# Cross-attention block in float32: pairs of fc split over a unit's border, with products joined in TensorE's accumulators

## The chip, the cores and the metric

The kernel runs on one core of a Trainium2 chip. The core has five engines that run side by side, each through its own list of instructions in order: TensorE (PE, matmuls into PSUM), VectorE (DVE), ScalarE (ACT), GpSimd (POOL) and SyncE (SP, which here issues most DMAs). They wait for each other by semaphores. The metric is the time of one execution on the device in microseconds; a profile, taken of one execution, shows what each engine did.

## The reference

Four batches of 512 rows of 512 numbers, all in float32. What is computed, with layer norm's affine part and all biases kept:

```python
x = layer_norm(hidden, ln1_w, ln1_b)
q = (x @ q_w + q_b)                      # 16 heads of 32
k, v = (enc @ k_w + k_b), (enc @ v_w + v_b)
attn = softmax(q @ k.T / sqrt(32))       # masked
hidden = hidden + (attn @ v) @ cproj_w + cproj_b
y = layer_norm(hidden, ln2_w, ln2_b)
y = gelu(y @ fc_w + fc_b)                # 512 -> 2048, tanh form
out = hidden + y @ proj_w + proj_b       # 2048 -> 512
```

## The kernel before, in words

The work has two stages. In the first, attention goes by *windows*: a window `w` is one batch and four heads (16 windows), and each has four *units*, one for each 128 queries, so there are 64 units; unit `u` is window `u // 4`, quarter `qt = u % 4`. A unit does `scores(w, qt)`: four matmuls on TensorE into one PSUM tile `sc` (L262), for each head a minimum on VectorE that copies the scores out (L266) and an exponential on ScalarE (L270). Then `turn(w, qt)`: transposes on VectorE (L285), and in odd units a reciprocal of the sums (L290), its copy `rr` on ScalarE (L292) and two more transposes (L293, L294). SyncE's DMAs exchange blocks of the result (L328), and some units later `attend` multiplies by the values (L345, tile `av`) and VectorE scales it (L350, `oT`). The tile `sc` has one buffer, so the next scores wait for the fourth minimum of the unit before.

Between these pieces stands other work, so that TensorE has something to do while VectorE and ScalarE are at the scores: projections for coming windows (`prep_k`, `prep_q`, `prep_v`: L218, L228, L240), the output projection `cproj` (L386), layer norms with their transposes (`tp`, L159), and the MLP of the batches 0 and 1. Which item follows which unit is written out by hand in the lists `first` and `later`: for a tuple, entry `qt` holds the items that follow the scores of that unit; for a list, the items are dealt over the window's four units by their costs. `some(n)` takes the next MLP items from the list `mlp`, in which a chain counts 1 and a pair 2. The program order of an engine is the order in which these Python functions are called.

The MLP's first product (`fc`) has two forms. `fc(b, f)` is a chain: four matmuls 128x512 into an accumulator, then gelu on ScalarE (L537), for 128 of the 2048 columns. Batch 1's first half of the columns goes this way (8 chains, in the units 57 to 63). `fc_by_pair(b, c)` takes two such column blocks at once by `fc_seven`: a 2x2 block product in seven half-width products in place of eight (Strassen's scheme in Winograd's form). Its inputs are sums of blocks: of the weights (`a_sums`, by POOL in the first stage through `fc_sums`, by VectorE in the second through `sum_wa`), and of the normed input (`y_sums`). Each product is two matmuls 128x256 (L495). Before, the seven products go to four accumulators, and the results are combined outside of PSUM: ScalarE copies the first product (L498), VectorE adds twice by 512, once by 256 and once more by 512 (L455), and ScalarE applies gelu to two blocks of 512 (L513).

The accumulators `acc` are a pool of four PSUM banks for everything in the first stage but `sc`. The second product `proj` (L554) multiplies by the lower weights and adds to `hid` on VectorE (L558). Weights of the MLP go through a ring of eight places that `load_mlp` refills when their last reader is done.

The second stage, `last_mlps`, has no attention left: half of batch 1's MLP, then batches 2 and 3, again by pairs, one directly after the other, with `project` for the second product, also by seven products (L622). There the four banks of `sc` have become a second pool (`half_tile`), and SyncE loads a pair's weights (`load_wa`, L578) when the pair before the last is done with the place.

ScalarE holds one table of functions at a time; where an exponential follows a gelu, or the reverse, a table load stands between them (ACT_TABLE_LOAD).

Of the kernel before, what the change touches and what calls it, by code (L numbers as in the profile page):

```python
# [20 lines left out]
P = 128  # L21
# [31 lines left out]
def xattn_block(ctx: ExitStack, tc: tile.TileContext, x, encT, mask, q_w, k_w, v_w, c_w, fc_w, p_w, vecs, rows, out):  # L53
# [342 lines left out]

    def load_hid(b, ts_):

        for t in ts_:
            if ("hid", b, t) not in S:  # L400
                S["hid", b, t] = hids.tile([P, D], F32, tag="hid", name=f"hid_{b}_{t}")
            Q[0].dma_start(out=S["hid", b, t], in_=S["xa", b][ts(t, P), :])
        for t in ts_:
            add_row(S["hid", b, t], 1)
# [46 lines left out]
    def sub(o, x0, x1, engine=None):  # L451
        (engine or nc.vector).tensor_tensor(o, x0, x1, ALU.subtract)  # L452

    def add(engine, o, x0, x1):
        engine.tensor_tensor(o, x0, x1, ALU.add)  # L455
# [16 lines left out]
    def y_sums(b):  # L472
        y11, y12, y21, y22 = y_blocks(b)
        e = nc.vector if b else nc.gpsimd
        sub(ys[:, 0], y12, y11)
        sub(ys[:, 1], y22, ys[:, 0])
        sub(y12, y22, y12, e)
        sub(ys[:, 2], y21, ys[:, 1], e)

    def acc_half(name):  # L480
        return acc_tile(name).rearrange("p (i l) -> p i l", i=2)

    def fc_seven(b, c, g, a, s, half):

        y11, t3, y21, y22 = y_blocks(b)
        t1, t2, t4 = (ys[:, i] for i in range(3))
        s1, s2, s3, s4 = s
        q1, q26 = (acc_half(f"{n}_{b}_{c}") for n in ("q1", "q26"))
        q57, q34 = (half(f"{n}_{b}_{c}") for n in ("q57", "q34"))
        p1 = small.tile([P, HL], F32, tag="p1", bufs=1, name=f"p1_{b}_{c}")  # L490
        g = g.rearrange("p i (j l) -> p (i j) l", j=2)

        def product(o, x, y):
            for k in range(2):
                nc.tensor.matmul(o, x[:, k], y[:, k], start=(k == 0), stop=(k == 1))  # L495

        product(q1[:, 0], a[0][:, 0:2], y11)
        nc.scalar.copy(p1, q1[:, 0])  # L498
        product(q26[:, 0], a[0][:, 2:4], y21)
        product(q26[:, 1], s2, t2)  # L500
        add(nc.vector, g[:, 0:4:3], q26, p1[:, None, :].broadcast_to([P, 2, HL]))
        product(q57[:, 1], s3, t3)
        product(q57[:, 0], s1, t1)
        u2 = g[:, 3:4]
        add(nc.vector, g[:, 1:3], q57, u2.broadcast_to([P, 2, HL]))
        add(nc.vector, g[:, 3], q57[:, 0], g[:, 2])
        product(q34[:, 0], s4, y22)
        product(q34[:, 1], a[1][:, 2:4], t4)
        add(nc.vector, g[:, 1:3], q34, g[:, 1:3])
        for i in range(2):  # L510
            f = 2 * c + i
            h = g[:, 2 * i : 2 * i + 2]
            nc.scalar.activation(h, h, AF.Gelu_apprx_tanh, bias=vec[:, FCB + f : FCB + f + 1], scale=1.0)  # L513

    fc_pairs = [(b, c) for b in range(SPLIT) for c in range(NP)]

# [3 lines left out]
    def fc_sums():  # L520

        while count[3] < len(fc_pairs) and count[3] < count[4] + 2:
            b, c = fc_pairs[count[3]]
            if ("fcw", b, 2 * c + 1) not in S:
                return
            x, y = raw_pair(b, c)
            s = wsum[:, count[3] % 2]
            a_sums(x[:, :2], x[:, 2:], y[:, :2], y[:, 2:], s[:, 0], s[:, 1], y[:, :2], s[:, 2], nc.gpsimd)
            S["ws", b, c] = s[:, 0], s[:, 1], y[:, :2], s[:, 2]
            count[3] += 1  # L530

    def fc(b, f):
        q, k = divmod(f, FQ)
        acc = acc_tile(f"accf_{b}_{f}")
        for d in range(ND):
            nc.tensor.matmul(acc, S["fcw", b, f][:, d, :], S["yT", b][:, d, :], start=(d == 0), stop=(d == ND - 1))  # L536
        nc.scalar.activation(  # L537
            gT[q % 2][:, k, :], acc, AF.Gelu_apprx_tanh, bias=vec[:, FCB + f : FCB + f + 1], scale=1.0
        )
        count[1] += 1  # L540
        load_mlp()

    def fc_by_pair(b, c):
        q, k = divmod(2 * c, FQ)
        fc_seven(b, c, gT[q % 2][:, k : k + 2, :], raw_pair(b, c), S["ws", b, c], acc_half)
        count[1] += 2
        count[4] += 1
        load_mlp()
        fc_sums()
# [40 lines left out]
    def last_mlps():  # L590
# [17 lines left out]
        def fc_pair(b, c, sums):  # L608
            sums()
            fc_seven(b, c, ga[:, c], [wa[c % 2][:, i] for i in range(2)],  # L610
                     [ws[c % 2][:, i] for i in range(4)], half_tile)

        def project(b, pairs, sums, turns, middle):
# [51 lines left out]
            for t in range(2):  # L665
                product(q4[t], g22, t4, (t,))
                add(nc.vector, hid(1, 0, t), q4[t][:, t], hid(1, 0, t))
                nc.sync.dma_start(out=out[b, ts(2 + t, P), :HL], in_=hid(1, 0, t))

        y_sums(SPLIT)  # L670

# [48 lines left out]
    def do(fn):  # L720
        return [(0.0, fn)]
# [19 lines left out]
    def FC(b, q):  # L741
        if b < SPLIT:
            return [(2 * CHAIN * 7 / 8, lambda c=c: fc_by_pair(b, c)) for c in range(q * FQ // 2, (q + 1) * FQ // 2)]
        return [(CHAIN, lambda f=f: fc(b, f)) for f in range(q * FQ, (q + 1) * FQ)]

# [71 lines left out]
    def some(n):  # L817
        taken = []
        while n > 0:
            n -= 1 if mlp[0][0] == CHAIN else 2  # L820
            taken.append(mlp.pop(0))
        assert n == 0
        return taken

    def hid_(b, *ts_):
        return do(lambda: load_hid(b, ts_))

# [15 lines left out]
    def norm(b, *ts_):  # L843
# [9 lines left out]
    first[5] = (  # L853
        [k] + stat(0, 0, 1, 2, 3) + rs(0) + do(fc_sums) + x3 + norm(0, 0, 1, 2, 3) + [v], [q] + t2 + do(lambda: y_sums(0)), some(2) + pb_(0), some(2)
    )
    k, q, v = A(9)
    x1, x2, x3, x4 = inputs(3)
    first[6] = [k, q] + some(4) + [v] + x1
    k, q, v = A(10)
    first[7] = [k, q] + x2[:1] + some(2) + x2[1:2] + some(2) + [v]  # L860

    k, q, v = A(11)
    first[8] = h_(1, 0, 1) + x2[2:] + [k, q] + x3[:2] + some(2) + x3[2:3] + [v] + x3[3:] + h_(1, 2, 3) + x4
    later[8] = cb(1) + C(1)
    k, q, v = A(12)
    first[9] = [q] + some(2) + [k] + some(2) + [v]
    k, q, v = A(13)
    first[10] = [k, q] + some(4) + [v]
    k, q, v = A(14)
    t2 = turns2(1)  # L870
    first[11] = (
        [k, q] + stat(1, 0, 1, 2, 3) + rs(1), some(2) + norm(1, 0, 1, 2, 3), some(1) + t2[:2] + [v],
        t2[2:] + pb_(1) + some(1) + h_(2, 2, 3, 0, 1)
    )

    k, q, v = A(15)
    c = C(2)
    first[12] = [k, q], cb(2) + [v], c[:2], c[2:]
    first[13] = some(1), some(1) + stat(2, 0, 1), some(1) + stat(2, 2, 3) + rs(2), some(2)
    first[14] = some(1) + norm(2, 0, 1), some(1) + norm(2, 2, 3), some(2), some(1)  # L880
    first[15] = hid_(1, 2, 3) + some(1), some(1), some(1), some(2)

    for w in range(NW):
        if w and w % NG == 0:
            make_mb(w // NG)

        work, rest = first[w], later[w]
        by_unit = isinstance(work, tuple)
# [88 lines left out]
```

## Time and profile before

| what | us |
|---|---|
| runs | 802.65, 802.84, 805.95 (median 802.84) |
| profiled execution, its own time | 801.93 |
| span in the profile | 800.2 |
| TensorE busy | 785.3 |
| VectorE busy | 573.8 |
| ScalarE busy | 339.5 |
| POOL busy | 123.9 |

The span runs from the first to the last instruction; the execution's time holds some 1.7 us around it. A line of the timeline gives start, duration, engine, source line, operation and tiles; lines of the same kind that follow each other are merged (x8 is a pass each of eight: a float32 matmul shows as two), and the bracket at the end tells of idle time before it and of what ended it. TensorE's ends are modelled, so starts are the safer reading: a pair's length is read from its start to the next item's start. A line of the waits gives who waited for whom, the total, how often and the longest. The first stage ends at about 549.6 us, where the first pair of the second stage starts. In a unit without disturbance the first minimum starts 1.21 after its scores, the first exponential 1.94, and the fourth ends 4.78 after them (units 20, 22, 25 and others).

### The profile page before, as it was taken

What the parts mean: (1) busy time and instruction counts of PE and PEld (TensorE: products, weight loads), DVE (VectorE), ACT (ScalarE), POOL (GpSimd) and SP (SyncE); (2) the same over time, 40 slices, a digit from 0 to 9 for tenths busy, and PEclk for the clock granted to TensorE, in tenths of its full rate; (3) what the DMA queues carried; (4) which work ended last, traced back from release to release, by engine and by line L of the source; (5) the groups of instructions that cost most, each with busy time, mean ns of one, the idle gap of its engine ahead of it and who ended that gap; (6) DMA issues with size and microseconds to landing.
All of it is one profiled execution on the core that took longest, in us unless ns stands there. A gap on an engine that the chain in (4) does not pass through costs nothing.

```text
span 800.2 us, 12085 instructions
## 1 busy us (share of the span) xinstructions
PE 785.3 (98%) x4178; PEld 499.4 (62%) x4178; DVE 573.8 (72%) x1179; ACT 339.5 (42%) x745; POOL 123.9 (15%) x146
## 2 busy tenths in 40 slices
PE   9999999989999999999999999999999999999998
PEld 6545455456655645556553433446888888888887
DVE  3789998888888857779878988546738983368511
ACT  2567765547763636456554479500201220022100
POOL 1210030055121141001220100020040020200011
PEclk9999999999999999999999999999999999999999
DMA  8889999847897777787777799882325330033001
GB/s 325 289 230 241 235 237 244 231 115 182 209 240 196 211 210 192 179 198 199 181 173 213 205 261 246 202 254 93 117 84 172 118 106 14 27 86 86 1 14 40
DMA packets 60957, 137.15 MB, mean 171 GB/s; under 512 B 12464, under 2 KB 15664, under 8 KB 60768
## 3 DMA queue, kind: packets, MB, share of 16 engines
q1 hardware_dynamic: 59472, 132.43, 61.3%
q0 software_dynamic: 896, 2.82, 1.1%
q10 hardware_dynamic: 528, 1.14, 0.7%
q8 instruction: 33, 0.54, 0.3%
q14 instruction: 28, 0.23, 0.1%
HBM read 58.22 MB, written 6.82 MB: 81 GB/s over the span
## 4 chain that ended last, share of the span: by engine, by line
PE 87%; DVE 6%; SPq 3%; ACT 1%; issue 1%; DMA 1%; POOL 0%; DVEq 0%; POOLq 0%; ACTq 0%
PE q L495 20%; PE accp L554 8%; PE sc L262 7%; PE accc L386 7%; PE av L345 7%; PE accv L240 6%; PE acck L218 6%; PE accq L228 5%; PE accf L536 3%; DVE ptt L266 3%; SPq L328 2%; PE q4p L622 2%; PE q3p L622 2%; PE q5p L622 2%; PE q6p L622 2%; PE q7p L622 2%
## 5 line engine op out<-in xcount | busy, mean ns | idle before, releaser
L270 ACT ACTIVATE ptt<-ptt,mn 128x512 f32<-128x512 f32 x256 | 181.7, 711 | 135.1 <-DVE mn L266 134.8
L266 DVE CUSTOM_DVE_ANT_0 ptt<-sc,mb 128x512 f32<-128x512 f32 x256 | 161.0, 685 | 32.7 <-PE sc L262 32.4
L285 DVE STREAM_TRANSPOSE tb<-ptt 128x1024 f32<-128x1024 f32 x96 | 119.2, 1242 | 14.4 <-ACT ptt L270 12.9
L554 PE MATMUL accp<-pbt,gt 128*128 128x512 f32 x192 | 86.7, 600 | 0.0
L495 PE MATMUL q<-yT,gt 128*128 128x256 f32 x320 | 78.9, 379 | 0.0
L262 PE MATMUL sc<-pbt 32*128 32x512 f32 x512 | 73.0, 640 | 4.7 <-DVE mn L266 2.5
L513 ACT ACTIVATE ga<-ga,vec 128x512 f32<-128x512 f32 x40 | 26.7, 714 | 93.2 <-DVE ga L455 93.2
L495 PEld LDWEIGHTS q<-yT,gt 128*128 128x128 f32 x320 | 60.8, 190 | 8.7 <-issue 0.5
L554 PEld LDWEIGHTS accp<-pbt,gt 128*128 128x128 f32 x192 | 35.2, 190 | 49.0 <-issue 46.4
L240 PEld LDWEIGHTS accv<-ptt,xe 128*128 128x128 f32 x512 | 58.7, 192 | 9.5 <-issue 6.7
L495 PE MATMUL q<-ys,gt 128*128 128x256 f32 x240 | 61.8, 380 | 0.5 <-DVE ys L452 0.5
L240 PE MATMUL accv<-ptt,xe 128*128 128x128 f32 x512 | 60.8, 277 | 0.0
L218 PE MATMUL acck<-xe,ptt 128*128 128x512 f32 x128 | 59.1, 605 | 0.0
L228 PE MATMUL accq<-xe,ptt 128*128 128x512 f32 x128 | 58.4, 599 | 0.0
L386 PE MATMUL accc<-wc,oT 128*128 128x512 f32 x128 | 56.6, 596 | 0.0
L495 PEld LDWEIGHTS q<-ys,gt 128*128 128x128 f32 x240 | 45.4, 190 | 7.4 <-DVE ys L452 0.9
L345 PE MATMUL av<-pT,v 128*32 128x256 f32 x768 | 48.1, 392 | 1.8 <-DMA gt<-tb 0.7
L498 ACT COPY p<-q 128x256 f32<-128x256 f32 x28 | 9.9, 355 | 92.5 <-PE q L495 92.5
L270 ACT ACTIVATION_READ_ACCUMULATOR ptt<-ptt,mn 128x1 f32 x256 | 47.8, 187 | 0.0
L252 POOL TENSOR_TENSOR v<-v,row 128x512 f32<-128x512 f32 x16 | 20.4, 1275 | 172.9 <-ACT v L245 172.8
L228 PEld LDWEIGHTS accq<-xe,ptt 128*128 128x128 f32 x128 | 23.6, 190 | 32.4 <-issue 30.4
L262 PEld LDWEIGHTS sc<-pbt 32*128 32x128 f32 x512 | 20.0, 182 | 37.9 <-issue 21.4
(137 smaller groups left out, 1071.4 us busy)
## 6 DMA issues: line engine op xcount, KB each, us to landing
pT<-tb SPq DMA_DIRECT2D x384, 136.0 KB, 2.4
pbt<-p_w_dram SPq DMA_DIRECT2D x40, 256.0 KB, 3.1
gt<-fc_w_dram SPq DMA_DIRECT2D x40, 256.0 KB, 2.6
gt<-tb SPq DMA_DIRECT2D x64, 136.0 KB, 3.4
xe<-tb SPq DMA_DIRECT2D x56, 136.0 KB, 3.1
pbt<-fc_w_dram SPq DMA_DIRECT2D x24, 256.0 KB, 3.9
ptt<-k_w_dram SPq DMA_DIRECT2D x16, 256.0 KB, 3.8
xe<-encT_dram SPq DMA_DIRECT2D x16, 256.0 KB, 4.6
```

Source lines behind the costliest of these rows:

```text
L218: nc.tensor.matmul(acc, S["wk", w][:, d, :], eT[:, d, :], start=(d == 0), stop=(d == ND - 1))
L228: nc.tensor.matmul(acc, S["wq", w][:, d, :], xT[:, d, :], start=(d == 0), stop=(d == ND - 1))
L240: nc.tensor.matmul(acc[:, ts(t, P)], eT[:, d, ts(t, P)], S["wv", w][:, d, :], start=(d == 0), stop=(d == ND - 1),)
L262: nc.tensor.matmul(sc[:, h, :], qT[r, ts(qt, P)], kT[r, :], start=True, stop=True)
L266: nc.vector.tensor_tensor_reduce(out=s, in0=sc[:, h, :], in1=S["mb", w // NG], scale=1.0, scalar=FMAX, op0=ALU.add, op1=ALU.min, accum_out=mn,
L270: nc.scalar.activation(s, s, AF.Exp, bias=mn, scale=-1.0, accum_out=sums[:, qt, h : h + 1])
L285: nc.vector.transpose(*two_heads[k])
L345: nc.tensor.matmul(av[ts(h, HD), : 2 * P].rearrange(shape, **kw), v[:, t, ts(h, HD)], p[t][h], start=(t == 0), stop=(t == NT - 1),)
L386: nc.tensor.matmul(acc, S["oT", b][:, g, ts(t, P)], wc[:, g, :], start=(g == 0), stop=(g == NG - 1))
L495: nc.tensor.matmul(o, x[:, k], y[:, k], start=(k == 0), stop=(k == 1))
L554: nc.tensor.matmul(acc, gT[q % 2][:, k, ts(t, P)], S["pw", b, q * FQ + k], start=(k == 0), stop=(k == FQ - 1))
L622: nc.tensor.matmul(o[:, t], a[:, c, ts(t, P)], w[:, c], start=(c == pairs[0]), stop=(c == pairs[-1]))
```

## The change

Three things are changed together.

1. In `fc_seven` three accumulators serve in place of four. Products that go to the same sum are joined by TensorE: `qb` takes s1 t1 and s3 t3, is copied by ScalarE to `g[:, 2:]` (L502 of the new file), and is then added to by s4 y22 and, in its other half, the product with t4; `qa` takes a11 y11, is copied by ScalarE to the quarter `u2` (L507), and is then added to by a12 y21. VectorE has one add of 256 (with `qc`) and one of 512 (with `qb`); POOL has two adds of 256; gelu goes in blocks of 256, 256 (directly from `qa`) and 512.
2. The function is a generator with one `yield`. In the first stage it makes two items: `fc_start` runs to the `yield` (four products), `fc_end` the rest (three products, and the copy to `u2` ahead of them). `some(n)` counts each as one, so that a pair can begin after the scores of one unit and end after those of the next. In the second stage both parts run one after the other.
3. The first half of batch 1's `fc` goes by pairs too (four pairs in place of eight chains), with POOL making their sums and `y_sums(1)`. The lists for the units 22 to 63 are written anew. By them `fc_end` is the first item after the scores in the units 23, 24, 26, 37, 38, 43, 44, 60 and 61; in 27, 58 and 62 a start and its end stand together behind the scores.

The core of the diff:

```diff
     def y_sums(b):
         y11, y12, y21, y22 = y_blocks(b)
-        e = nc.vector if b else nc.gpsimd
-        sub(ys[:, 0], y12, y11)
-        sub(ys[:, 1], y22, ys[:, 0])
-        sub(y12, y22, y12, e)
-        sub(ys[:, 2], y21, ys[:, 1], e)
+        e, o = ((nc.vector, nc.gpsimd), (nc.gpsimd,) * 2)[b] if b <= SPLIT else (nc.vector,) * 2
+        sub(ys[:, 0], y12, y11, e)
+        sub(ys[:, 1], y22, ys[:, 0], e)
+        sub(y12, y22, y12, o)
+        sub(ys[:, 2], y21, ys[:, 1], o)
...
-        q1, q26 = (acc_half(f"{n}_{b}_{c}") for n in ("q1", "q26"))
-        q57, q34 = (half(f"{n}_{b}_{c}") for n in ("q57", "q34"))
-        p1 = small.tile([P, HL], F32, tag="p1", bufs=1, name=f"p1_{b}_{c}")
+        qb, qa, qc = half(f"qb_{b}_{c}"), acc_half(f"qa_{b}_{c}"), acc_half(f"qc_{b}_{c}")
...
-        product(q1[:, 0], a[0][:, 0:2], y11)
-        nc.scalar.copy(p1, q1[:, 0])
-        product(q26[:, 0], a[0][:, 2:4], y21)
-        product(q26[:, 1], s2, t2)
-        add(nc.vector, g[:, 0:4:3], q26, p1[:, None, :].broadcast_to([P, 2, HL]))
-        product(q57[:, 1], s3, t3)
-        product(q57[:, 0], s1, t1)
-        u2 = g[:, 3:4]
-        add(nc.vector, g[:, 1:3], q57, u2.broadcast_to([P, 2, HL]))
-        add(nc.vector, g[:, 3], q57[:, 0], g[:, 2])
-        product(q34[:, 0], s4, y22)
-        product(q34[:, 1], a[1][:, 2:4], t4)
-        add(nc.vector, g[:, 1:3], q34, g[:, 1:3])
-        for i in range(2):
+        product(qb[:, 0], s1, t1, True)
+        product(qb[:, 1], s3, t3)
+        nc.scalar.copy(g[:, 2:], qb)
+        product(qa[:, 0], a[0][:, 0:2], y11, True)
+        product(qc[:, 0], s2, t2, True)
+        add(nc.gpsimd, g[:, 3], g[:, 2], g[:, 3])
+        yield
+        nc.scalar.copy(u2, qa[:, 0])
+        add(nc.vector, u2, qc[:, 0], u2)
+        add(nc.gpsimd, g[:, 3], g[:, 3], u2)
+        product(qb[:, 0], s4, y22)
+        product(qb[:, 1], a[1][:, 2:4], t4)
+        add(nc.vector, g[:, 1:3], qb, u2[:, None, :].broadcast_to([P, 2, HL]))
+        product(qa[:, 0], a[0][:, 2:4], y21)
+        for i, o, x in ((0, g[:, 1], g[:, 1]), (0, g[:, 0], qa[:, 0]), (1, g[:, 2:], g[:, 2:])):
...
     def FC(b, q):
-        if b < SPLIT:
-            return [(2 * CHAIN * 7 / 8, lambda c=c: fc_by_pair(b, c)) for c in range(q * FQ // 2, (q + 1) * FQ // 2)]
-        return [(CHAIN, lambda f=f: fc(b, f)) for f in range(q * FQ, (q + 1) * FQ)]
+        parts = []
+        for c in range(q * FQ // 2, (q + 1) * FQ // 2):
+            parts += [(CHAIN, lambda c=c: fc_start(b, c)), (CHAIN * 3 / 4, lambda c=c: fc_end(b, c))]
+        return parts
...
     first[5] = (
-        [k] + stat(0, 0, 1, 2, 3) + rs(0) + do(fc_sums) + x3 + norm(0, 0, 1, 2, 3) + [v], [q] + t2 + do(lambda: y_sums(0)), some(2) + pb_(0), some(2)
+        [k] + stat(0, 0, 1, 2, 3) + rs(0) + do(fc_sums) + x3 + norm(0, 0, 1, 2, 3) + [v], [q] + t2 + do(lambda: y_sums(0)),
+        some(1) + pb_(0), some(2)
     )
     k, q, v = A(9)
     x1, x2, x3, x4 = inputs(3)
-    first[6] = [k, q] + some(4) + [v] + x1
+    first[6] = some(1) + [k], [q] + some(1), some(1) + [v], some(2) + x1
...
-    first[13] = some(1), some(1) + stat(2, 0, 1), some(1) + stat(2, 2, 3) + rs(2), some(2)
+    first[13] = (
+        do(lambda: y_sums(1)) + c[2:], some(1) + stat(2, 0, 1), some(2) + stat(2, 2, 3) + rs(2), some(1)
+    )
     first[14] = some(1) + norm(2, 0, 1), some(1) + norm(2, 2, 3), some(2), some(1)
-    first[15] = hid_(1, 2, 3) + some(1), some(1), some(1), some(2)
+    first[15] = hid_(1, 2, 3) + some(2), do(lambda: hid_rows(1, (2, 3))) + some(1), some(2), some(1)
```

## The prediction

> **What bounds the kernel now.** I read three views: the page's busy shares with its chain, the waits of TensorE, and the timeline of single units (a unit is one `scores` and `turn`, 64 in all).
>
> ```profile
> span 800.2 us, 12085 instructions
> PE 785.3 (98%) x4178; PEld 499.4 (62%) x4178; DVE 573.8 (72%) x1179; ACT 339.5 (42%) x745; POOL 123.9 (15%) x146
> ...
> PE 87%; DVE 6%; SPq 3%; ACT 1%; issue 1%; DMA 1%; POOL 0%; DVEq 0%; POOLq 0%; ACTq 0%
> ```
>
> ```profile
> PE tp L159 <- ACT pbt L231: 3.0, 1, 3.0
> PE sc L262 <- DVE mn L266: 2.5, 2, 1.6
> PE sc L262 <- ACT pbt L231: 2.2, 2, 1.4
> PE warm L775 <- POOL nhalf L766: 1.4, 1, 1.4
> PE av L345 <- DMA gt<-tb: 0.7, 1, 0.7
> PE av L345 <- ACT p L498: 0.7, 1, 0.7
> PE q L495 <- DVE ys L452: 0.5, 1, 0.5
> PE av L345 <- issue: 0.3, 1, 0.3
> PE q1p L622 <- ACT ga L513: 0.2, 1, 0.2
> ```
>
> TensorE (PE) does nothing for only 11.5 us in all, and most of that lies ahead of unit 22 (176.90 us), where the layout is unchanged. From there to the end its gaps are 0.69, 0.30, 0.90, 0.45 and 0.24: 2.6 us in 623. So the time is TensorE's work plus its waits, one for one; what VectorE (DVE) or ScalarE (ACT) save is worth nothing, and what they make TensorE wait for is paid in full. The next view is the timeline of unit 25, which holds a whole pair.
>
> ```profile
> 202.28 1.14 PE L262 MATMUL sc<-pbt 32*128 32x512 f32 x8
> 203.35 1.99 PE L495 MATMUL q<-yT,pbt 128*128 128x256 f32 x8
> 204.23 0.72 ACT L270 ACTIVATE ptt<-ptt,mn 128x512 f32<-128x512 f32 x1 [1.15 <-DVE mn L266]
> 205.18 1.03 PE L495 MATMUL q<-ys,wsum 128*128 128x256 f32 x4
> ...
> 206.36 0.71 ACT L270 ACTIVATE ptt<-ptt,mn 128x512 f32<-128x512 f32 x1
> ...
> 207.43 0.40 ACT L292 COPY rr<-rsum 128x256 f32<-128x256 f32 x1 [0.27 <-DVE rsum L290]
> 207.74 0.36 ACT L498 COPY p<-q 128x256 f32<-128x256 f32 x1
> ...
> 209.59 1.93 PE L345 MATMUL av<-pT,v 128*32 128x256 f32 x32
> ```
>
> See where ScalarE's copy of the first product stands: q1 is complete 2 us after the scores begin, but its copy (L498) ends at 208.10, that is scores + 5.82, because ScalarE takes its list in order and the unit's four exponentials and the copy `rr` stand ahead of it. Today TensorE does not care: the seven products go to four accumulators, and none is written again after it is read.
>
> **The change, part by part.**
>
> *Products saved.* Four pairs of batch 1 take seven half-width products in place of two chains. Behind scores a pair takes 209.59 - 203.35 = 6.24; two chains (L536) run from 468.22 to the next `av` at 475.28, 7.06. Saved: 4 x 0.82 = 3.3 us, all on TensorE.
>
> *Gaps that go.* The 0.69 (unit 23) and 0.30 (unit 27) belong to the old order, and the 0.45 to `y_sums(1)` on DVE, which moves to GpSimd (POOL) in unit 52, over 40 us ahead of its reader in unit 58: -1.4 us.
>
> *The new wait.* Now TensorE adds a second product into qb and into qa, each in place of a separate accumulator. The first may come only when ScalarE has copied qb (L502), the other only when it has copied qa to `u2` (L507). L502 is issued in `fc_start`; L507 stands behind the `yield`, so it is issued with `fc_end`. Where `fc_end` is the first work of a unit, `scores` has been issued before it: L507 stands in ScalarE's list behind that unit's four exponentials (and, in odd units, behind `rr`), just where L498 stands in the rows above. Those rows price it. In undisturbed even units (22) L498 ends at scores + 5.13, in odd ones (25) at + 5.82. TensorE needs it after the scores and two products, at 205.18 - 202.28 = 2.90. The wait is 2.23 in an even unit and 2.92 in an odd one; nothing else is queued on TensorE that could go first, since it takes its matmuls in order, and `av`, the next scores and their DVE work all stand behind it.
>
> Where the items fall, by the layout: `fc_end` opens units 23, 37, 43, 61 (odd) and 24, 26, 38, 44, 60 (even): 4 x 2.92 + 5 x 2.23 = 22.8. In units 27, 58 and 62 start and end stand together. There the copy of qb is what is late: it begins where L498 did and takes 0.58 (the 128x512 copy of `v`, L245, has 577 ns), so it ends at + 6.04 (odd) or + 5.36 (even), and TensorE wants it after four products, at + 4.63: 1.4 + 0.7 + 0.7 = 2.8. Together 25.7 us.
>
> *Lag on top.* These prices hold where DVE and ScalarE are free when the scores come. They are not in five places, each priced by unit rows of before. Unit 22 is now 4.6 us long but its DVE work ends at + 6.1, so unit 23 starts 0.3 late. Unit 59 shrinks in the same way: 0.75 in unit 60. Units 53 to 57 hold `accp`, statistics and norms as before, where DVE fell behind (the first minimum of units 54 to 58 came 3 to 4.7 us after its scores, against 1.21): a start 2.5 late in unit 58, and 0.4 more than the old 0.90 gap ahead of it. Unit 62 follows the short unit 61, whose adds, three gelus and table load (0.42 + 0.69 + 0.36 + 0.36 + 0.71 + 1.28 from + 6.6) end 3.7 after its scores, where the exponentials want 1.94: 1.8. Sum 5.7.
>
> *What costs nothing.* DVE loses some 1.4 us a pair (0.66 + 0.69 + 0.42 + 0.69 against 0.42 + 0.69), POOL gains two adds of 0.73: neither is on the path. The next items' accumulators are released by an `oT` or an earlier add, which are done. In the last stage pairs follow each other with no exponentials: the copy of qb is done about 2.4 after the pair's start and wanted at 3.46, so nothing waits. What is new there is that the first product reads `s1`, and both loads of the next weights now wait for the pair's end:
>
> ```profile
> 614.09 0.90 SPq L679 DMA_DIRECT2D pbt<-p_w_dram  x2
> 615.44 4.64 SPq L578 DMA_DIRECT2D gt<-fc_w_dram  x2
> 616.42 0.42 DVE L455 TENSOR_TENSOR gt<-gt 128x256 f32<-128x256 f32 x1
> ```
>
> Today `s1` of a pair that starts at 619.56 is summed from 616.42, 2.9 into the pair before; half a microsecond more for the second issue and the other load, and the same again for sharing, gives 3.9 + 0.42 = 4.3 against 6.05: 1.7 spare. I take 0; the ends are -0.5 and, if every one of 20 pairs comes 0.5 late, + 10. Splitting at the border adds at most one exposed weight load (0.19) per end, 2.3 in all; something always follows the scores and pays it, so I take 0.
>
> *Sum.* The profiled execution took 801.9 (span 800.2). 801.9 - 3.3 - 1.4 + 25.7 + 5.7 = 828.6. The median of the runs shown, 802.84, is 0.1% above that execution: forecast 829.
>
> **Two rules of the skill.** What a wait of this length does to the clock shows once:
>
> ```profile
> 172.68 0.66 PE L159 MATMUL tp<-ident,xn 128*128 128x128 f32 x4 [3.05 <-ACT pbt L231]
> 173.35 3.61 PE L345 MATMUL av<-pT,v 128*32 128x256 f32 x32
> 176.90 1.14 PE L262 MATMUL sc<-pbt 32*128 32x512 f32 x8
> ```
>
> After a gap of 3.05 between transposes, `av` took 3.61 in place of 1.93: about 1.7 us lost. The gaps of 0.69 to 1.63 elsewhere did no such thing. The Trainium skill, TensorE: Matmul & The Clock Gate, Part 1, says that the clock halves after an idle window of about 3.4 us that runs free, and Part 4 that transposes do not count as busy; by it my waits, between real matmuls, stay just under the window, and the sum has none of this. By the row alone, five waits of 2.9 to 3.6 could cost 5 x 1.7 = 8.5.
>
> The table load rows are 1.28 each, and the exponential follows at once (212.84 + 1.28, next row 214.14). The Trainium skill, ScalarE: Activation LUTs, What ACT_TABLE_LOAD costs, adds a drain of about 1.38 to every switch; by it unit 62 alone would lose some 1.4 more. The rows show no such drain, and the sum goes by the rows.
>
> **Rivals.** *The border hides the waits:* ScalarE reaches the copies before TensorE needs them, and only the saved work is left: 801.9 - 4.7 = 797, faster. For it: a unit's border lies between the first products and the second, and at nine of twelve ends the copy of qb is indeed done. It decides if the waits sum to less than 4.7 us, that is 0.4 per end; against it, L507 would have to end 2.2 us earlier than L498 ever did in a unit of before. *The waits also drop the clock or feed a lag* (L498 in unit 23 ended at + 8.02 where gelu's tables came in between): five ends at 1.7 to 2.2 more, 837 to 840; for it the row at 173.35, against it that the new waits mostly lie between dense matmuls. *The last stage waits for its weights as well:* 829 + 10 = 839; against it the 1.7 spare.
>
> **How the numbers follow.** Forecast 0.75, hidden waits 0.07, clock or lag 0.10, last stage 0.05, and 0.03 for something near no change. Low end: no lag, and every copy directly behind the exponentials (9 x 2.23 + 3 x 0.7 = 22.2) gives 819.4; 818 with the runs' scatter. High end: the clock or lag rival with a little of the last stage, 842. A measurement of this kernel can tell about 0.5% from no change. Faster by more than that 0.07, within it 0.03, slower 0.90.
>
> **What would show it.** Right: TensorE's waits list `q L498 <- ACT gt L507` with 9 entries near 2 to 3 us and a few for L502, some 30 us in all; the units that `fc_end` opens longer by that; ScalarE's L507 at scores + 5.1 or + 5.8; the last stage as long as before. Wrong: PE's idle time after 177 us still under 5 us, or waits on DMA or `gt` sums (L459) among the pairs of the last stage.

## The result and the profile after

The changed kernel took 851.74 us (median of 4 runs, 851.34 to 853.16) against 803.79 for the kernel before (4 runs, 802.65 to 805.95): a ratio of 1.0596, 95% interval 1.0568 to 1.0625. It is slower, as forecast, but by 48 us where I had 26, and outside my range of 818 to 842. Its profiled execution took 851.34, of which the span is 849.5. First the page of the kernel after: busy time of the engines, the clock granted to TensorE in 40 slices of the span (9 is full speed), and the shares of the chain of work that ended last.

```profile
span 849.5 us, 12272 instructions
PE 799.3 (94%) x4226; PEld 516.5 (61%) x4226; DVE 541.1 (64%) x1127; ACT 359.7 (42%) x809; POOL 187.8 (22%) x230
...
PEclk9999999989999998998999998999999999999999
...
PE 76%; DVE 9%; SPq 7%; ACT 4%; DMA 2%; issue 2%; POOL 0%; DVEq 0%; POOLq 0%
```

TensorE's share of the chain fell from 87% to 76%, and ACT rose from 1% to 4%. TensorE is now busy for 799.3 us, 14 more than before, although 3.3 us of products were taken out. The row of the clock says why: four slices show an 8, and in them matmuls are slower. TensorE's waits in the kernel after (total, number of times, longest):

```profile
PE qa L498 <- ACT gt L507: 22.1, 9, 2.9
PE qb L498 <- ACT gt L502: 7.2, 4, 4.6
PE av L345 <- DVE yT L162: 3.6, 1, 3.6
PE sc L262 <- DVE mn L266: 3.4, 3, 1.6
...
PE av L345 <- DMA pT<-tb: 2.2, 1, 2.2
```

The first line is the one that I had asked for: nine waits on the copy to `u2`, 22.1 us in all. With every line of this view TensorE is idle for 46.7 us against 11.5 before. The last stage is as long as it was: from its first pair (598.76) to the end 250.7 us, before 250.6. So all of the loss lies in the units 22 to 63.

One of the nine, unit 37, in the timeline of TensorE and then of ScalarE:

```profile
315.75 1.14 PE L262 MATMUL sc<-pbt 32*128 32x512 f32 x8
...
317.79 1.03 PE L498 MATMUL qb<-ys,pbt 128*128 128x256 f32 x4
321.62 2.07 PE L498 MATMUL qa<-yT,pbt 128*128 128x256 f32 x4 [2.81 <-ACT gt L507]
323.49 1.91 PE L498 MATMUL qb<-ys,wsum 128*128 128x256 f32 x4
```

```profile
321.20 0.37 ACT L507 COPY gt<-qa 128x256 f32<-128x256 f32 x1
```

The copy ends at 321.57, 5.82 after the scores: it stands behind the four exponentials and `rr`, as the prediction had it. What I had not counted is to the right of the gap: the product that ends it takes 2.07 in place of 1.03, and the next one 1.91. The same stretch cut at every 3.41 us, with each engine's busy time, its number of instructions in brackets, and then the granted clock:

```profile
core 0: us, PE busy (x) PEld busy (x) DVE busy (x) ACT busy (x) POOL busy (x), PEclk, DMA share, GB/s
317.41:320.83 3.42, 1.41 (x7) 0.90 (x5) 3.41 (x11) 2.93 (x8) 0.00 (x0) 1.00 0.78 204
320.83:324.24 3.41, 2.62 (x6) 2.17 (x7) 2.47 (x5) 2.73 (x6) 0.73 (x1) 0.50 0.00 0
324.24:327.65 3.41, 3.41 (x9) 2.69 (x9) 0.00 (x0) 1.21 (x3) 0.00 (x0) 0.50 0.46 154
327.65:331.07 3.42, 3.42 (x43) 2.01 (x42) 0.00 (x0) 1.36 (x2) 0.72 (x1) 1.00 0.00 0
```

TensorE worked 1.41 us of the first window, and then had half its clock for two. The kernel after has ten such half-clock windows (from 174.06, 187.71, 201.36, 320.83 for two, 382.27 for two, 508.56, 525.63 and 539.28), the kernel before had one (from 173.44).

### The profile page after: what moved, and what is told of

The parts are those of the page before. It is cut to its first block, busy times and chain, and to the rows that moved or that the text cites. A ratio compares the mean times of both kernels' runs of the same rounds, so it can differ in the third digit from the quotient of the medians.

```text
span 849.5 us, 12272 instructions
## 1 busy us (share of the span) xinstructions
PE 799.3 (94%) x4226; PEld 516.5 (61%) x4226; DVE 541.1 (64%) x1127; ACT 359.7 (42%) x809; POOL 187.8 (22%) x230
## 4 chain that ended last, share of the span: by engine, by line
PE 76%; DVE 9%; SPq 7%; ACT 4%; DMA 2%; issue 2%; POOL 0%; DVEq 0%; POOLq 0%
PE qb L498 11%; PE accp L552 8%; PE accc L386 7%; PE qa L498 6%; SPq L328 6%; PE av L345 6%; PE sc L262 6%; PE acck L218 5%; PE accv L240 5%; PE accq L228 4%; DVE ptt L266 4%; PE qc L498 3%; ACT ptt L270 2%; PE q5p L620 2%; PE q3p L620 2%; PE q7p L620 2%
## 5 line engine op out<-in xcount | busy, mean ns | idle before, releaser
L459 POOL TENSOR_TENSOR ga<-ga 128x256 f32<-128x256 f32 x40 | 30.1, 753 | 121.5 <-ACT ga L502 84.4
L502 ACT COPY ga<-qb 128x512 f32<-128x512 f32 x20 | 11.7, 586 | 101.4 <-PE qb L498 58.2
L498 PE MATMUL qa<-yT,pbt 128*128 128x256 f32 x96 | 31.3, 457 | 22.1 <-ACT gt L507 22.1
L516 ACT ACTIVATE ga<-ga,vec 128x256 f32<-128x256 f32 (+1 forms) x40 | 24.3, 609 | 61.7 <-DVE ga L459 61.7
L459 POOL TENSOR_TENSOR gt<-gt 128x256 f32<-128x256 f32 x24 | 17.4, 725 | 123.3 <-ACT gt L502 63.3
L218 PEld LDWEIGHTS acck<-xe,ptt 128*128 128x128 f32 x128 | 24.2, 198 | 32.5 <-issue 29.6
L228 PEld LDWEIGHTS accq<-xe,ptt 128*128 128x128 f32 x128 | 23.2, 190 | 33.4 <-issue 30.5
L350 DVE TENSOR_TENSOR oT<-av,pT 128x256 f32<-128x256 f32 x24 | 10.1, 422 | 52.2 <-PE av L345 49.3
```

The lines of the kernel that those rows point to most:

```text
L218: nc.tensor.matmul(acc, S["wk", w][:, d, :], eT[:, d, :], start=(d == 0), stop=(d == ND - 1))
L228: nc.tensor.matmul(acc, S["wq", w][:, d, :], xT[:, d, :], start=(d == 0), stop=(d == ND - 1))
L498: nc.tensor.matmul(o, x[:, k], y[:, k], start=clear and k == 0, stop=k == 1, skip_group_check=not clear)
```

## The experiments

**Theory.** The products that TensorE adds into an accumulator behind a copy tie it to ScalarE's list, and the gaps that this makes also halve its clock. **Rivals:** the new lists (what follows which unit, and the extra work on VectorE and GpSimd) cost the time by themselves; or the gaps cost only themselves and something else slowed the matmuls.

All runs in one table. "Idle" is the sum of TensorE's waits, "half" the number of half-clock windows. The column "sum" is 800.2 (the span before) plus the idle time over 11.5, plus 1.7 for each half window over one (the two runs with idle time, below, give this price; a window that is partly idle costs less), less 3.3 for the saved products where batch 1 goes by pairs, plus 15.5 of filling matmuls in the kernel that has them.

| kernel | median, us | ratio (95%) | idle | half | sum | span |
|---|---|---|---|---|---|---|
| the change | 851.74 | 1.0596 (1.0568 to 1.0625) | 46.7 | 10 | 847.4 | 849.5 |
| u2_early | 834.34 | 1.0397 (1.0347 to 1.0448) | 36.2 | 8 | 833.5 | 832.3 |
| fill | 845.52 | 1.0511 (1.0461 to 1.0561) | 32.4 | 4 | 838.4 | 842.0 |
| split_new | 824.47 | 1.0266 (1.0248 to 1.0284) | 28.1 | 4 | 818.6 | 819.0 |
| old_seven | 830.15 | 1.0320 (1.0297 to 1.0343) | 33.8 | 5 | 826.0 | 826.1 |
| join_only | 816.72 | 1.0154 (1.0132 to 1.0175) | 22.9 | 2 | 813.3 | 814.9 |
| split_old | 808.53 | 1.0065 (1.0040 to 1.0089) | 18.3 | 3 | 807.1 | 806.9 |
| split_joined | 816.09 | 1.0160 (1.0137 to 1.0184) | 22.1 | 4 | 812.6 | 812.6 |
| norm_late | 802.41 | 0.9987 (0.9974 to 1.0001) | 12.4 | 2 | 802.8 | 802.1 |
| split_old_late | 806.45 | 1.0043 (1.0027 to 1.0059) | 17.7 | 2 | 804.8 | 804.6 |
| split_joined_late | 812.10 | 1.0104 (1.0084 to 1.0123) | 19.7 | 4 | 810.2 | 809.8 |

The sums come within 2.1 us of the spans, except in `fill` (3.6). Three things thus account for nearly all of the time: idle TensorE, half-clock windows, and products. This is bookkeeping: it says where the time went, and the experiments say why.

### The copy taken ahead of the border (u2_early)

```diff
         product(qc[:, 0], s2, t2, True)
         add(nc.gpsimd, g[:, 3], g[:, 2], g[:, 3])
-        yield
         nc.scalar.copy(u2, qa[:, 0])
+        yield
         add(nc.vector, u2, qc[:, 0], u2)
```

> The changed kernel with one line moved: ScalarE's copy of qa to u2 stands ahead of the yield, so in the unit of fc_start and ahead of the next unit's exponentials. My theory (the waits for ScalarE's copies, and half-clock windows that these waits bring about, 9 of them in the changed kernel): the nine waits for L507, 22.1 us in all, go, and with them eight of the nine half-clock windows after unit 22, some 1.7 us each; the waits for L502 stay. 851.7 - 22.1 - 13.6 = 816. Rival 1 (the clock falls for other reasons, such as the new lists or the load of the engines): the waits go and the windows stay, 829.6. Rival 2 (the waits only move to another engine's turn): over 840.

Measured: 834.34 against 816 expected: 17 of the 48 us come back. The waits on L507 are gone, but others took their place. TensorE's waits of this kernel:

```profile
PE qb L498 <- ACT gt L502: 12.7, 4, 5.1
PE qa L498 <- DVE gt L459: 4.9, 4, 1.4
```

The waits on L502 grew in two of the contiguous pairs, from 1.45 to 2.59 in unit 27 and from 0.80 to 5.14 in unit 62; unit 58 waits 4.6 in both kernels. The order inside these pairs is that of the change, but the unit ahead is shorter (unit 61 lasts 3.86 us in place of 7.88), so ScalarE comes late to the next exponentials and the copy behind them. And where the gaps were, the next accumulator is now asked for before VectorE has read it (second line). The wait was partly passed on, which my 816 had not allowed for. Seven extra half-clock windows were left as well: none behind an L507, five behind L502 in the units 27, 58 and 62, and two in unit 47.

### Matmuls in the gap (fill)

```diff
         product(qb[:, 1], a[1][:, 2:4], t4)
         add(nc.vector, g[:, 1:3], qb, u2[:, None, :].broadcast_to([P, 2, HL]))
+        if fill:
+            spare = acc_half(f"spare_{b}_{c}")
+            for _ in range(fill):
+                nc.tensor.matmul(spare[:, 0], a[1][:, 2], t4[:, 0], start=True, stop=True)
         product(qa[:, 0], a[0][:, 2:4], y21)
```

Four extra matmuls, whose result nobody reads, stand ahead of the waiting product in the nine ends that open a unit.

> The changed kernel with work added: in the nine ends that stand alone behind scores, four more matmuls 128x256 into an accumulator that nobody reads, right ahead of the product that waits for u2. Its results are not used; the output is unchanged. My theory: the wait still ends when ScalarE's copy ends, but TensorE is busy for 1.73 us of it, so less than 1.2 us of each stay idle, the half-clock windows that follow them go (eight of nine) and the time falls by 8 x 1.7 = 13.6 to 838, although 36 matmuls (15.6 us) more are done. Rival 1 (the clock falls for other reasons): the windows stay and the time is 852. Rival 2 (the added matmuls delay what comes behind): 852 to 867.

Measured: 845.52, 7.5 above the 838 expected, but faster than the change although it does 36 matmuls more (36 x 0.43 = 15.5 us). TensorE's waits of this kernel:

```profile
PE qb L498 <- ACT gt L502: 8.7, 4, 4.6
PE qa L498 <- ACT gt L507: 6.5, 9, 1.2
```

The nine waits fell from 22.1 to 6.5, which is the 15.5 us of matmuls that stand in them: by itself an even exchange. What made it faster is that only four half-clock windows remain, six fewer than in the change, and 6 x 1.7 = 10 us. None of the four stands behind an L507. The intervals keep the gain unsharp (the spans differ by 7.5, and this is the kernel whose sum is furthest off), but the sign is what the clock predicts, and a price of the gaps alone has no room for it.

### Idle time of two lengths, by itself (idle_short, idle_long)

To measure the clock apart from the change: in the kernel before, each of the 20 pairs of the last stage waits once for ScalarE, behind its seventh product. ScalarE copies an accumulator (and copies the copy some times), and TensorE does one matmul on it that nobody reads.

```diff
+        if idle is not None:
+            junk = small.tile([P, HL], F32, tag="p1", bufs=1, name=f"junk_{b}_{c}")
+            nc.scalar.copy(junk, q34[:, 1])
+            for _ in range(idle):
+                nc.scalar.copy(junk, junk)
+            nc.tensor.matmul(q1[:, 1], junk[:, :P], junk, start=True, stop=True)
```

`idle` is 2 in the one and 5 in the other.

> The kernel before with a wait put behind each of the 20 pairs of the second stage: ScalarE copies a quarter of the last product, copies that copy twice, and TensorE does one matmul 128x256 on it whose result is overwritten unread. It measures how long an idle stretch must be before the clock halves. By the rows of the changed kernel, in which a 3.41 us window of a fixed grid with 2.11 us or more of idle time was followed by a half-clock window and one with 2.00 was not, gaps of about 1.4 us (a start of 0.7 and two copies of 0.36) bring no half-clock window at all: 800 + 20 x (1.4 + 0.43) = 837, clock 1.00. Rival (any repeated gap of this kind lowers the clock): over 850.

> As idle_short with five further copies in place of two, so gaps of about 2.5 us. My theory (2.0 to 2.1 us of idle time in one window of 3.41 on a fixed grid is enough): a gap of 2.5 lies in one window with at least 2.05 of it in (3.41 - 2.5 + 2 x 0.45) / 3.41 = 0.53 of the cases, so about 10 half-clock windows, up to 1.7 us each: 800 + 20 x 2.93 + 10 x 1.5 = 874. Rival (a whole window must be idle, as I reckoned in the prediction): no half-clock window, 859.

Measured: 841.92 and 890.23 (one run each), against 837 and 874 expected. The waits of the first, and of the second:

```profile
PE q L514 <- ACT junk L513: 26.7, 20, 1.3
```

```profile
PE q L514 <- ACT junk L513: 52.9, 20, 2.6
```

Twenty gaps of 1.3 bring no half-clock window, as expected; twenty of 2.6 bring thirteen, where I had expected ten. The spans are 840.1 and 888.5: 48.4 apart, of which the gaps are 26.2. The other 22.2 over thirteen windows is 1.71 for each, half of 3.41 as it should be. So gaps between dense matmuls do halve the clock, and well below a whole window. A gap is also a little dearer than its length: the first kernel's span is 39.9 above that of before, of which the gaps are 26.7 and the twenty matmuls 8.6, and the other 4.6, some 0.2 a gap, stand in no line of the waits.

### The joining taken out, the new lists kept (split_new)

`fc_seven` has the four accumulators of before again, with the `yield` behind the third product; lists, sums and items are those of the change. So one product of each pair also moves across the border, and VectorE gets back the adds that the change had given to GpSimd (584.2 us busy against 541.1).

```diff
         product(q26[:, 1], s2, t2)
         add(nc.vector, g[:, 0:4:3], q26, p1[:, None, :].broadcast_to([P, 2, HL]))
+        yield
+        q57, q34 = (half(f"{n}_{b}_{c}") for n in ("q57", "q34"))
         product(q57[:, 1], s3, t3)
```

> The changed kernel with its lists, sums on POOL and items split at the border as they are, and only the joining taken out: each pair again uses four accumulators (three products in fc_start, four in fc_end) and no product waits for a copy. If joining is the cause, TensorE's waits on L502 and L507 go (29.3 us) and most of the half-clock windows with them; what stays is what the new lists brought in the changed kernel (yT 3.6, the exchange's DMA 2.2, some VectorE lag) and perhaps two to four half-clock windows of 1.7: 800.2 - 3.3 + 6 + 3 to 7 = 806 to 810 of span, a time of 808 to 812. Rival: the new lists cost most by themselves, as the kernel with the lists and unsplit pairs suggests (830): then 825 to 832, with waits of av on the exchange's DMA and of sc on the minimum of 5 us and more each.

Measured: 824.47, between the two (808 to 812, and 825 to 832), and close to the rival. The change is 30.5 us longer in its span, and that is what joining costs under these lists: 18.6 of idle time and six half-clock windows (10.2) are most of it. It can be read unit by unit. In the units 24, 26, 27, 37, 38, 43, 44 and 61 the change waits 2.12, 2.12, 1.45, 2.81, 2.12, 2.81, 2.12 and 2.81, which is 18.4; this kernel waits 0 to 0.3 there. But it is itself 19 us above the span of before, which I had put at 6 to 10. Its waits:

```profile
PE sc L262 <- DVE mn L266: 5.0, 4, 1.9
PE av L345 <- ACT p L501: 3.9, 2, 2.2
PE av L345 <- issue: 3.6, 1, 3.6
PE av L345 <- DMA pT<-tb: 3.2, 4, 2.2
```

These stand, for the most part, in the units 23 (2.24), 47 (4.17), 58 (2.59), 60 (4.27), 62 (2.19) and 63 (1.57). In 23, 58 and 60 the change idles too, for 2.93, 5.49 and 2.58, but mostly at the copies: there one wait took the other's place. So the two prices don't add up from single removals. In units as short or as full as the new lists make them, work that TensorE reads soon is late by itself. In the units 23 and 47 it is the exchange (for unit 47 see the account of the prediction below). In 58 and 62 `av` waits for `p`, the copy of the first product: without joining, too, a bank is free for the next tile only when ScalarE has come to the copy out of it. For the 3.6 of unit 60 the profile names no releaser, but the trace's semaphore times do: `av` starts 0.10 after VectorE's add of 256 ends (500.73), and this add stands in VectorE's list behind the unit's minima and transposes.

### The old pairs whole under the new lists (old_seven)

The pair as it was before, all of it where `fc_start` stands, and nothing at `fc_end`:

```diff
-        started[b, c] = fc_seven(b, c, gT[q % 2][:, k : k + 2, :], raw_pair(b, c), S["ws", b, c], acc_half)
-        next(started[b, c])
+        fc_seven(b, c, gT[q % 2][:, k : k + 2, :], raw_pair(b, c), S["ws", b, c], acc_half)
...
     def fc_end(b, c):
-        list(started[b, c])
```

> The changed kernel with the old fc_seven (four accumulators, nothing joined) in the new lists: fc_start does all seven products and fc_end only the counting and the loads. My theory: no waits for copies are left and no half-clock windows from them; the new lists keep their own waits (3.6 for yT ahead of av, 2.2 for an exchange DMA, 1.1 for sums), 802 - 3.3 + 7 = 806. Rival (the lists of the units 22 to 63 are what costs): well over 820.

Measured: 830.15, a miss by 24 us, and the first sign that the lists cost something themselves. It isn't a clean removal, since the units of `fc_end` become short: unit 44 lasts 4.84 us in place of 9.81, and in unit 45 `av` then waits 4.12 for the exchange (8.2 in all). `split_new` is the cleaner one.

### The joining alone, under the lists of before (join_only)

The lists, chains and sums of before, with the new `fc_seven` run whole in each pair.

```diff
     def fc_by_pair(b, c):
         q, k = divmod(2 * c, FQ)
-        fc_seven(b, c, gT[q % 2][:, k : k + 2, :], raw_pair(b, c), S["ws", b, c], acc_half)
+        list(fc_seven(b, c, gT[q % 2][:, k : k + 2, :], raw_pair(b, c), S["ws", b, c], acc_half))
```

> The kernel before with the new fc_seven alone, each pair whole in its old place, batch 1 by chains, old lists. My theory: the joined accumulators cost by themselves, since the fifth product waits for the copy of qb, which stands behind the unit's exponentials: by the unit rows of before 0.7 in units 22, 1.4 in 25 and 33, 1.5 in 26 and 37, 1.7 in 45, 3.6 in 23 where gelu's tables come in between, nothing in 42: 11.8 us of waits, one of them long enough for a half-clock window (1.7), so 803 + 13.5 - 1 = 815. Rival (only the split at the border costs): 803.

Measured: 816.72, close to the 815 expected: joining by itself, under the old lists, costs 1.5%. The longest line of its waits is one that before has not:

```profile
PE qb L494 <- ACT gt L498: 9.1, 7, 2.2
```

Here the copy is that of `qb` (L502 of the change), which stands behind the exponentials whenever a whole pair follows the scores. That the total fits so well is in part luck: I had 11.8 for this line, and it has 9.1; 2.1 more of waiting on VectorE's sums (L452 and L455), which I had not counted, make up for it.

### Batch 1 by pairs, under the lists of before (split_old, split_joined)

`split_old`: batch 1's first half goes by pairs of the old form, split in two items; its sums and `y_sums(1)` go to GpSimd. Nothing is joined, and the lists change in one place.

```diff
-        return [(CHAIN, lambda f=f: fc(b, f)) for f in range(q * FQ, (q + 1) * FQ)]
+        parts = []
+        for c in range(q * FQ // 2, (q + 1) * FQ // 2):
+            parts += [(CHAIN, lambda c=c: fc_start(b, c)), (CHAIN, lambda c=c: fc_end(b, c))]
+        return parts
...
-    first[13] = some(1), some(1) + stat(2, 0, 1), some(1) + stat(2, 2, 3) + rs(2), some(2)
+    first[13] = do(lambda: y_sums(1)) + some(1), some(1) + stat(2, 0, 1), some(1) + stat(2, 2, 3) + rs(2), some(2)
```

> The kernel before with one part of the change alone, without joined accumulators: batch 1's first half of fc by pairs in the old form, in the places of the old chains, each pair as two items (three products and the first add; four products and the rest), y_sums(1) and the weight sums on POOL. Nothing on TensorE is written twice, so no wait for a copy. Theory (in the units 54 to 63 VectorE is already 2 to 4 us behind, so the 9.8 us of adds that it gets come back in part as waits of the scores for the minimum): 3.8 saved, about as much given back, 804. Rival (the saved products count in full): 800.

`split_joined` is the same with the joined form for batch 1, the copy to `u2` ahead of the border:

```diff
-        started[b, c] = fc_seven(b, c, gT[q % 2][:, k : k + 2, :], raw_pair(b, c), S["ws", b, c], acc_half)
+        started[b, c] = (fc_joined if b else fc_seven)(b, c, gT[q % 2][:, k : k + 2, :], raw_pair(b, c), S["ws", b, c], acc_half)
```

> As split_old, but batch 1's pairs by the joined form with the copy to u2 ahead of the yield; batch 0 keeps the old form and the old lists. Theory (joining spares VectorE 1.35 us a pair but makes TensorE wait where the copy of qb stands behind gelus): four pairs with 1 to 3 us each of waits for L502 or for an accumulator that a late add frees, 3.8 saved: 803 - 3.8 + 8 = 807, slower than split_old. Rival (with the copies ahead of the border the joined form costs nothing): 800, faster than split_old.

Measured: 808.53 and 816.09, each slower than expected. In `split_old` it is VectorE that falls behind:

```profile
PE sc L262 <- DVE mn L266: 7.2, 4, 2.7
```

Before, this line has 2.5. A chain gave VectorE nothing; a pair gives it adds, in the units 57 to 63, right behind batch 2's statistics and norms (units 53 to 57). Two of the waits that follow, 2.71 and 2.32 long, were each followed by a half-clock window. The 3.3 us are saved (without them the sum would be 810.4, and the span is 806.9), but 6.8 of waiting and 3.4 of clock outweigh them. In `split_joined` one add that an accumulator waits for (5.6) comes on top.

### Room made for VectorE (norm_late, split_old_late, split_joined_late)

Batch 2's statistics and norms move out of the units 53 to 57 to the pairs of the last stage, where VectorE has time:

```diff
+                if b == SPLIT:
+                    for t in {4: (0, 1), 5: (2, 3)}.get(c, ()):
+                        stat2(b + 1, t)
+                    if c == 5:
+                        ln_rs((2, b + 1))
+                    for t in {6: (0, 1), 7: (2, 3)}.get(c, ()):
+                        norm2(b + 1, t)
...
-    first[13] = some(1), some(1) + stat(2, 0, 1), some(1) + stat(2, 2, 3) + rs(2), some(2)
-    first[14] = some(1) + norm(2, 0, 1), some(1) + norm(2, 2, 3), some(2), some(1)
+    first[13] = some(1), some(1), some(1), some(2)
+    first[14] = some(1), some(1), some(2), some(1)
```

`norm_late` is the kernel before with this alone, the other two are `split_old` and `split_joined` with it.

> The kernel before with that edit alone: statistics and norms of batch 2 in the second stage, fc of batch 1 by chains as before. Theory: only the 0.90 us wait of unit 58 goes, 802, no measurable change; so what split_old_late gains over this is the saved products. Rival (the second stage feels the norms): 804 to 806.

> split_old with one more edit: batch 2's statistics and norms, 4.9 us of VectorE's work in the units 53 to 57, are done in the second stage beside batch 1's last pairs. Theory (what ate the saved products in split_old was VectorE's lag in the units 54 to 63, 5.6 us more waits of TensorE and two half-clock windows): the lag starts from 0 and the 3.3 us saved, the 0.45 of y_sums and the 0.90 of unit 58 are kept, 798 to 800, faster than the kernel before by about 0.5%. Rival (the pairs' adds alone keep VectorE behind in the units 58 to 63, or the norms delay the second stage): 804 or more.

> split_joined with the same edit. If its waits (5.6 for an accumulator that a late add frees, 3.4 for the copy of qb) came from VectorE's lag, they go and it is as fast as split_old_late, 798 to 800; if they come from joining itself (the copy of qb behind gelus and exponentials), 3 to 6 us of them stay, 802 to 806.

Measured: 802.41, 806.45 and 812.10. Alone the edit makes no difference that can be told. It relieves the other two by 2 us, which is within the intervals, and by 4, far less than I had expected (798 to 800 for both): in `split_old_late` the lag is all but gone from the units 55 to 57, but the units 60 to 63 still start their minima 3.8 to 5.2 after the scores (1.8 to 3.9 in `norm_late`, 1.21 undisturbed): that points to the pairs' own adds, which no run takes away by themselves. No version was faster than the kernel before by an amount that can be told.

## Why the prediction was right in part and wrong in size

- **What bounds.** Right: TensorE's work plus its waits, one for one. The sums in the table rest on this and hold within 2.1 us in all but one kernel.
- **The new wait.** Right, and nearly exact. The nine ends: forecast 22.8, measured 22.1. In undisturbed even units L507 ends at scores + 5.13, in odd ones at + 5.82 to + 5.94, as L498 did before. `u2_early`, where the copy stands ahead of the border, and `split_new`, where nothing is copied there, have no such line.
- **Contiguous pairs and lag.** 2.8 and 5.7 forecast, 8.5; measured 7.2 behind L502 and 1.1 behind an add (L459), 8.3. That the totals agree is luck, since the parts fell differently: unit 58 lost 5.49 with its scores' wait, where I had 3.6 (0.7 + 2.9), and unit 62 0.8, where I had 2.5. Unit 61 was itself 7.88 long by its own wait, which left time for the adds and gelus ahead of unit 62; in `u2_early`, where unit 61 lasts 3.86, unit 62 waits 5.14.
- **Saved products.** Right: 3.3 forecast. TensorE's busy time, less 1.7 for each half-clock window, is 783.6 before, 780.1 in `split_old` and 780.2 in `split_old_late`.
- **The last stage.** Right: 250.7 against 250.6. The loads of its weights cost nothing.
- **The clock.** This step failed. The prediction wrote that the waits "stay just under the window, and the sum has none of this". Nine more half-clock windows came, up to 9 x 1.7 = 15.3 us, the greater part of the 22.6 by which the span missed (849.5 against 828.6 - 1.7 = 826.9); another 5.2 is idle time that the sum did not have (35.2 more than before, 30.0 forecast). The row that I had in hand, `av` at 3.61 behind a gap of 3.05, spoke for it; I set the rule of the Trainium skill, TensorE: Matmul & The Clock Gate, Part 1 (half speed after an idle window of about 3.4 us), above it. The measurement differs from that rule: 2.0 us of idle time in a window is enough. My rival had the mechanism, at five places; the chance that I gave it, 0.10, was too low, and its number too.
- **The old form.** The prediction wrote of the four accumulators that "TensorE does not care" when the copy comes. It does where the next tile needs the bank: before, that cost 0.7 (the line `av` behind `p` L498 in the prediction's waits), and in `split_new` 3.9.
- **The new lists.** The prediction priced where the pair's items fall and what VectorE does late, but not what else the lists move. Two waits come from that, and both are `av` waiting for the exchange: 2.2 in unit 29 and 3.6 in unit 47. For unit 47 the profile names another releaser, the copy `yT` on VectorE:

```profile
412.82 10.04 SPq L328 DMA_DIRECT2D pT<-tb  x16
423.51 0.77 DVE L162 TENSOR_SCALAR yT<-tp,vec 128x512 f32<-128x512 f32 x1
425.06 1.93 PE L345 MATMUL av<-pT,v 128*32 128x256 f32 x32 [3.56 <-DVE yT L162]
```

  But `yT` is done at 424.28, 0.78 too early. The trace has the landings of the sixteen DMAs of the exchange: the last is issued at 422.28 and lands at 424.65, and `av` starts 0.41 later. In `u2_early` and `split_new` it starts 0.41 after that landing too; before, the last one landed at 395.45, and `av` stood at 395.87 without a wait. The lists brought this about from both sides: the sixteen start 4.10 after the scores of unit 46 (before: 2.44), since VectorE is later there, and TensorE is through with its other work sooner. With 0.9 more on the minimum these waits are 6.7 us. `split_new` shows that the lists' own price is larger than what can be seen beside the copies: 19 us of span without any joining.
- **What stays open.** 2.1 us of the span have no place in my sum. It counts a gap at its length, and by `idle_short` a gap costs some 0.2 more; whether this is the rest wasn't tested.

The rival by which the border hides the waits is out: at the border ScalarE is at the exponentials, and no L507 in a unit's opening `fc_end` came before scores + 5.1.

## What to carry to other kernels

An accumulator that is copied out and then added to again puts the copying engine's list into TensorE's path: before joining products there, look up where in that list the copy stands at the moment when TensorE wants the bank, and keep a free bank if anything long is ahead of it. Price a new wait on TensorE twice, by its length and by the half-speed window that it may bring; below about 1.8 us of idle time in a window it costs little more than itself here, and several gaps of 2 to 3 us cost up to 1.7 each on top. And when one removal doesn't give the time back, look at which other wait stands in the same unit: waits that end at the same place hide each other. The profile's name for a wait is also worth a check against the end of the work that it names: here the one named was done 0.78 us too early, and it was a DMA.

## What the runs showed of the hardware

In each trace all half-clock stretches start on one grid of 3.41 us, and what decided in these kernels is how long TensorE was idle in a window of this grid. Over all fourteen kernels, of the windows at full clock, 51 that were idle for 2.01 us or more were each followed by a half-clock one; of 25 that were idle for 1.5 to 1.85 none was, nor any with less; of 10 between, three were. The threshold in these kernels is thus near 0.57 of a window (TensorE's ends are modelled, so the edge can't be had sharper), where the Trainium skill, TensorE: Matmul & The Clock Gate, Part 1, speaks of a whole idle window. A borderline pair from the kernel after, in the columns of the window view above:

```profile
249.15:252.56 3.41, 1.41 (x4) 0.34 (x2) 3.38 (x7) 0.99 (x2) 0.00 (x0) 1.00 0.93 221
252.56:255.98 3.42, 3.20 (x41) 1.70 (x42) 0.85 (x4) 0.00 (x0) 2.83 (x5) 1.00 0.35 121
```

It was as busy (1.41) as the window at 317.41, and the one behind it kept its clock. Because the kernel is not bound to the grid, a gap of 2 to 3 us falls in one window or across two: six of the nine waits of 2.1 to 2.9 behind L507 were followed by a half-clock window, and three were not. Even the 3.56 of unit 47 brought none in the change, where it left 1.73 idle in one window and 1.83 in the next; in `fill` nearly the same wait (3.53) left 2.62 in one window and brought one. A half-clock window that is itself idle for 0.76 us or more was followed by another one in each of the eight cases seen; between 0.6 and 0.75 both occurred.
